# Two post-norm layers on one core: the mLSTM's gates on four column groups, its state parts first, and eight heads' scores on four row groups

## The chip, the cores and the metric

One core of a Trainium2 chip runs the whole program. The metric is the device time in microseconds; the time quoted for a kernel is the median of its runs. A profile is one execution, recorded instruction by instruction. PE is TensorE's matmuls, PEld its weight loads, DVE VectorE, ACT ScalarE, POOL GpSimd and SP the sync engine, which issues most DMAs here. L69 means line 69 of the kernel before.

## The reference

Input x is 4 x 256 tokens of 256 features. Four sub-layers follow, each as `x = layernorm(x + f(x))`: softmax attention with 16 heads and rotary parts; a gated network of width 1024 with a Walsh-Hadamard transform; an mLSTM block that has a gated network inside; and a gated network with int8 weights. The change touches the third:

```python
q, k, v = h_in @ wq, h_in @ wk, h_in @ wv        # h_in = rmsnorm(x) * norm1_w; 8 heads, dqk 16, dv 32
i_pre, f_pre = softcap(h_in @ w_ig + b_ig), softcap(h_in @ w_fg + b_fg)   # cap 15, tanh
Fcum = cumsum(log_sigmoid(f_pre))
Dmat = Fcum[s] - Fcum[t] + i_pre[t], and -inf where t > s
m = max_t(Dmat)
C = (q @ k.T) / sqrt(dqk) * exp(Dmat - m)
n = max(|sum_t C|, exp(-m))
h = (C / n) @ v                                   # per head, then an RMS norm per head
x1 = x + (sigmoid(o_pre) * h_norm) @ w_out
out = x1 + (silu(h2 @ w_gate) * (h2 @ w_up)) @ w_down     # h2 = rmsnorm(x1) * norm2_w
```

## The kernel before

All arithmetic of this part is fp32. The 1024 tokens are worked in two halves of 512 (two batches of 256 each), called n = 0 and 1, so that one half's mLSTM ("mixing phase") runs beside the other half's gated network.

The program is written in order, and the order written is a priority: at compile time a scheduler puts each engine's instructions in a fixed order, taking the first written one that is ready in its own reckoning. Each engine then runs its list in order and waits on semaphores. `issue_after(x)` keeps an instruction behind x on x's engine.

The interleaving is written with generators. `merge(first, other)` runs the mixing phase; where it yields a number of microseconds, that much of the other half's network is written in between. The network (`glu`, `down`) yields 1.7 after each piece of TensorE work: 16 such units in `glu` (a gate or an up product of 128 hidden rows), then 8 in `down`, 24 in all. These units are called filler below. What remains of them is written after the next norm.

PSUM has eight banks. The networks take turns on four ("d"), the mixing phase on the other four ("m").

A mixing phase, `mlstm(n)`:

- `mlstm_in` normalises (9.0 us of filler meanwhile), transposes to feature-major `fm`, and computes the gate pre-activations `w_if` (L69, from L622): gate g and batch bb give 32 output columns each, batch bb on PSUM partitions 32 bb to 32 bb + 31, gate g in columns of its own. Two tanh instructions follow, then `gates`: log-sigmoid, scans and maxima on ACT and DVE. The running maximum `gmax` is stored to DRAM as `far` (L689, SP).
- Queries and keys (`w_qk`), then four products for values and output gate (`w_vo`), then `by_token` (L704), which transposes the gate rows into `tok`, and keys by token (`ks`).
- `within(t, bb, half)`, four times: loads `far` of four heads, broadcast to all partitions, as `wide` (L740, SP, 512 KB), computes scores for four heads with 32-row matmuls on two row groups (L747) into two banks, subtracts `wide` from the mask on POOL (L756), takes eight exponentials on ACT (L763), and multiplies scores and exponentials on DVE (L767).
- `between` (L714, L726): the state that the first 128 tokens of a batch leave to the second, in two matmuls.
- `attend` (L778), a half behind: exponentials times values; an ACT copy and a DVE add take it out of PSUM.
- `head_norm`, once a batch: a chain of some twenty small steps on ACT and DVE that ends with `xs` (L808).
- The result is transposed and multiplied by `w_out` (L850), and L851 adds the residual. The next network's norm follows, with 6.0 us of filler, then its transposes, and then what is left of the filler.

Of the kernel before, what the change touches and what calls it, by code (L numbers as in the profile page):

```python
# [9 lines left out]
F32 = mybir.dt.float32  # L10
# [3 lines left out]
ALU = mybir.AluOpType  # L14
AX = mybir.AxisListType

P = 128
# [21 lines left out]
def tile_two_layers(ctx: ExitStack, tc: tile.TileContext, a: dict, out: bass.AP):  # L39
# [6 lines left out]
    def bank(tag):  # L46
        return psum.tile([P, 512], F32, tag=tag, name=f"ps_{tag}")
# [18 lines left out]
    def mm_k(ps, lhs, rhs, n):  # L66

        for i in range(n):
            nc.tensor.matmul(ps, lhsT=lhs(i), rhs=rhs(i), start=(i == 0), stop=(i == n - 1))  # L69

# [398 lines left out]
    nc.sync.dma_start(w_if[:, :, 0:40], a["w_if"])  # L469
    b_if = late.tile([64, 2], F32, tag="b_if", name="b_if")  # L470
    nc.gpsimd.memset(b_if, 0.0)
    for bb in range(2):
        for g in range(2):
            nc.sync.dma_start(b_if[32 * bb : 32 * bb + H1, g : g + 1], a["b_if"][32 * g : 32 * g + H1, :])
    vecs = load("vecs", [P, 6])
# [53 lines left out]
    def transposed(src, dst, tag, weight=None):  # L529
# [11 lines left out]
        return evicted  # L541

    def glu(xT, wg, wu, hT, tag):

        for c in range(NH):
            cols = slice(c * P, (c + 1) * P)
            pg, pu = bank(tag), bank(tag)
            mm_k(pg, lambda i: wg[:, i, cols], lambda i: xT[:, i, :], KC)
            yield 1.7
            mm_k(pu, lambda i: wu[:, i, cols], lambda i: xT[:, i, :], KC)  # L550
            g = work.tile([P, HALF], F32, tag="glu_g", name="glu_g")
            nc.scalar.activation(g, pg, AF.Tanh, scale=0.5)  # L552
            nc.vector.scalar_tensor_tensor(g, g, 1.0, pg, ALU.add, ALU.mult)
            nc.vector.tensor_tensor(hT[:, c, :], pu, g, ALU.mult)
            yield 1.7

    def down(hT, wd, j, tag, rows):

        po = bank(tag)[:, :D]
        for i in range(NH):  # L560
            nc.tensor.matmul(  # L561
                po, lhsT=hT[:, i, j * P : (j + 1) * P], rhs=wd[:, i, :], start=(i == 0), stop=(i == NH - 1)
            )
            if i == NH // 2 - 1:
                yield 1.7
        nc.vector.scalar_tensor_tensor(rows, po, 0.5, rows, ALU.mult, ALU.add)
        yield 1.7
# [35 lines left out]
    nc.gpsimd.memset(ones, 1.0)  # L603
    bias = mix.tile([2 * 32, 2], F32, tag="bias", name="bias")
    nc.scalar.mul(bias, b_if, 1.0 / CAP)
# [7 lines left out]
    def mlstm_in(n, t):  # L613
# [7 lines left out]
        pg = bank("m")  # L621
        for g in range(2):  # L622
            for bb in range(2):
                mm_k(
                    pg[32 * bb : 32 * bb + 32, g * S : (g + 1) * S],
                    lambda i: w_if[:, i, 32 * g : 32 * g + 32],
                    lambda i: fm[:, i, bb * S : (bb + 1) * S],
                    KC,
                )
        gt = mix.tile([64, 2, S], F32, tag="gt", name="gt")  # L630
        for g in range(2):
            nc.scalar.activation(
                gt[:, g, :], pg[:64, g * S : (g + 1) * S], AF.Tanh,
                bias=bias[:, g : g + 1], scale=1.0 / CAP,
            )
        gates(n, t, gt)
        yield 0.0
        pq, pk = bank("m"), bank("m")
        mm_k(pq, lambda i: w_qk[:, i, 0, :], lambda i: fm[:, i, :], KC)
        mm_k(pk, lambda i: w_qk[:, i, 1, :], lambda i: fm[:, i, :], KC)  # L640
        qT = mix.tile([P, HALF], F32, tag="qT", name=f"qT{n}")
# [5 lines left out]
        nc.gpsimd.memset(va[:, :, :, DV1], 1.0)  # L647
        sig = mix.tile([P, NJH, D], F32, tag="sig", name=f"sig{n}")
        for j in range(NJH):
            pv = bank("m")  # L650
            mm_k(pv, lambda i: fm[:, i, j * P : (j + 1) * P], lambda i: w_vo[:, i, :], KC)
            nc.scalar.copy(va[:, j, :, 0:DV1], pv[:, 0:D].rearrange("p (h d) -> p h d", h=H1))
            nc.scalar.activation(sig[:, j, :], pv[:, D:], AF.Tanh, scale=0.5)
        t.update(va=va, sig=sig, qT=qT, kT=kT)
        yield 1.0
        by_token(n, t)
        pt = bank("m")
# [16 lines left out]
    def gates(n, t, gt):  # L674
# [6 lines left out]
        neg = mix.tile([64, 1], F32, tag="neg", name="neg", bufs=2)  # L681
        nc.scalar.activation(lsp, gt[:, 1, :], AF.Exp, scale=-CAP)
        nc.scalar.activation(lsp, lsp, AF.Ln, bias=1.0)
        nc.vector.tensor_tensor_scan(fcum, ones, lsp, 0.0, ALU.mult, ALU.subtract)
        nc.vector.scalar_tensor_tensor(g, gt[:, 0, :], CAP, fcum, ALU.mult, ALU.subtract)
        nc.vector.tensor_tensor_scan(gmax, g, g, -3.0e38, ALU.max, ALU.max)
# [48 lines left out]

    def within(t, bb, half):


        wide = mix.tile([P, HG, S], F32, tag="wide", name="wide", bufs=2)
        nc.sync.dma_start(wide, t["far"][bb, half * HG : (half + 1) * HG].partition_broadcast(P))  # L740
        ps = (bank("m"), bank("m"))
        for odd in range(2):
            for c in range(2):
                for k in range(2):
                    rows = slice(32 * (2 * half + k), 32 * (2 * half + k) + 32)
                    tok = slice(bb * S + c * P, bb * S + (c + 1) * P)
                    nc.tensor.matmul(  # L747
                        ps[k][:, (2 * odd + c) * P : (2 * odd + c + 1) * P],
                        lhsT=t["kT"][rows, odd, tok], rhs=t["qT"][rows, tok],
                        start=True, stop=True,  # L750
                    )
        out = []
        for k in range(2):
            h = 4 * half + 2 * k
            ex = mix.tile([P, 4, P], F32, tag="ex", name="ex", bufs=4)
            nc.gpsimd.tensor_tensor(  # L756
                ex, mask.unsqueeze(1).to_broadcast([P, 4, P]),
                wide[:, 2 * k : 2 * k + 2, :].rearrange("p h (c s) -> p (h c) s", c=2), ALU.subtract,
            )
            for odd in range(2):  # L760
                for c in range(2):
                    at = 32 * bb + h + odd
                    nc.scalar.activation(  # L763
                        ex[:, 2 * odd + c, :], ex[:, 2 * odd + c, :], AF.Exp,
                        bias=t["tok"][:, c, 0, at : at + 1],
                    )
            nc.vector.tensor_tensor(  # L767
                ex, ps[k].rearrange("p (x s) -> p x s", x=4), ex, ALU.mult
            )
            out.append(ex)  # L770
        return out

    def attend(t, bb, half, exs, part, hv):

        ph = bank("m")
        for c in range(2):
            for x in range(HG):
                nc.tensor.matmul(  # L778
                    ph[:, (c * HG + x) * DV : (c * HG + x + 1) * DV],
                    lhsT=exs[x // 2][:, 2 * (x % 2) + c, :], rhs=t["va"][:, 2 * bb + c, half * HG + x, :],  # L780
                    start=True, stop=True,
                )
        heads = slice(half * HG, (half + 1) * HG)
        by_h = ph[:, : 2 * HG * DV].rearrange("p (c h d) -> p c h d", c=2, h=HG)
        nc.scalar.copy(hv[:, 0, heads, :], by_h[:, 0])
        nc.vector.tensor_tensor(hv[:, 1, heads, :], by_h[:, 1], part[:, heads, :], ALU.add)

    def head_norm(n, t, bb, hv):
# [18 lines left out]
        )  # L807
        nc.vector.scalar_tensor_tensor(  # L808
            hos[n][:, 2 * bb : 2 * bb + 2, :], t["sig"][:, 2 * bb : 2 * bb + 2, :], 1.0,
# [3 lines left out]
    def run(stream):  # L813
        for _ in stream:
            pass

    def take(count, stream):
        return itertools.islice(stream, count)

    def mlstm(n):  # L820

        t, waiting = {}, []

        def finish():
            bb, half, exs, hv = waiting.pop()
            attend(t, bb, half, exs, t["part", bb], hv)
            if half == 1:
                head_norm(n, t, bb, hv)

        yield from mlstm_in(n, t)  # L830
        for bb in range(2):
            hv = mix.tile([P, 2, H1, DV], F32, tag="hv", name="hv", bufs=2)
            for half in range(2):
                exs = within(t, bb, half)
                if half == 0:
                    carried = between(t, bb)
                run(take(1, carried))
                yield 1.5
                if waiting:
                    finish()  # L840
                waiting.append((bb, half, exs, hv))
        yield 3.0
        finish()
        yield 6.0
        fm = feature_major(n)
# [273 lines left out]
```

## Time and profile before

| | |
|---|---|
| median of 3 runs | 731.13 us (730.96 to 732.91) |
| the profiled execution | 732.8 us |
| its span | 731.0 us |
| granted TensorE clock | 0.997 of full |
| busy: PE, PEld | 719.4, 485.1 us |
| busy: DVE, ACT, POOL | 398.8, 238.8, 175.1 us |
| mixing phase 0, first gate matmul to the next network | 492.97 to 557.47 us |
| mixing phase 1, the same | 571.14 to 636.09 us |

A row of the order of time has the start, the length, the engine, the line, the operation, what it writes and reads, the shape and how many records were merged into it. In brackets stand the idle time ahead of it and what ended that. A matmul's modelled end overlaps the next one's start, so a row's true share is the distance to the next row's start. The rows that the prediction rests on are shown there.

### The profile page before, as it was taken

Reading aid. Unit: us, or ns where it says so; the run is one execution under the profiler, and the core shown is the slowest. Engines: PE = TensorE matmul, PEld = TensorE weight load, DVE = VectorE, ACT = ScalarE, POOL = GpSimd, SP = SyncE. Lnnn points to the kernel's source line nnn. Section 1 sums busy time; section 2 is a strip of 40 time slices with the busy share of each in tenths; the row PEclk is TensorE's granted clock in tenths of the full one; section 3 lists DMA queues with packets and bytes.
Section 4 is the critical chain, followed back from the end, with each engine's and each line's share of the span. In section 5 each row is a group of like instructions: output and inputs, shape, how many; then the busy total and the mean of one; then the engine's idle time right before and its main releaser. Section 6 shows DMA issues by size and latency. Waiting matters only on the chain.

```text
span 731.0 us, 8563 instructions
## 1 busy us (share of the span) xinstructions
PE 719.4 (98%) x2956; PEld 485.1 (66%) x2956; DVE 398.8 (55%) x1017; ACT 238.8 (33%) x625; POOL 175.1 (24%) x187
## 2 busy tenths in 40 slices
PE   8999999999999999999999999999999999999995
PEld 4667667667767767766766774655776476747885
DVE  0373544545655364364455555373778458754766
ACT  2232422432342242243233332126521452111553
POOL 0812422439440341243044000002300050000210
PEclk9999999999999999999999999999999999999998
DMA  8542042183133223322311313002130020000001
GB/s 247 212 107 56 18 123 56 25 279 61 29 101 58 44 87 59 62 79 48 72 30 30 58 60 66 0 1 64 55 115 1 23 94 1 0 1 0 1 1 57
DMA packets 48107, 45.34 MB, mean 62 GB/s; under 512 B 9504, under 2 KB 42688, under 8 KB 46016
## 3 DMA queue, kind: packets, MB, share of 16 engines
q1 hardware_dynamic: 46928, 40.47, 21.1%
q0 software_dynamic: 432, 3.15, 1.2%
q10 hardware_dynamic: 704, 1.18, 0.5%
q8 instruction: 23, 0.38, 0.2%
q14 instruction: 20, 0.16, 0.1%
HBM read 25.61 MB, written 1.08 MB: 37 GB/s over the span
## 4 chain that ended last, share of the span: by engine, by line
PE 91%; DVE 4%; ACT 2%; DMA 1%; issue 1%; POOL 0%; DVEq 0%; ACTq 0%
PE ps_mm L69 37%; PE ps_d L69 11%; PE ps_ot L69 8%; PE ps_m L69 8%; PE ps_d L561 5%; PE ps_pt L232 4%; PE ps_sc L232 4%; PE ps_d L861 4%; PE ps_sc L241 2%; PE ps_m L561 2%; PE ps_m L778 2%; PE ps_pt L241 2%; PE ps_mm L185 1%; DMA w_qkv<-in_w_qkv 1%; PE ps_m L534 1%; ACT ex L763 1%
## 5 line engine op out<-in xcount | busy, mean ns | idle before, releaser
L69 PE MATMUL ps_mm<-xT,w_qkv 128*128 128x512 f32 x248 | 115.8, 593 | 0.0
L176 POOL TENSOR_TENSOR rope_raw<-rope_raw,cst 128x512 f32<-128x512 f32 x32 | 40.7, 1271 | 231.8 <-DVE rope_swp L173 224.5
L260 ACT ACTIVATE pr<-ps_sc,nmax 128x256 f32<-128x256 f32 x64 | 29.5, 472 | 142.2 <-DVE nmax L251 142.2
L69 PEld LDWEIGHTS ps_mm<-xT,w_qkv 128*128 128x128 f32 x248 | 47.0, 190 | 37.2 <-issue 33.8
L69 PEld LDWEIGHTS ps_ot<-prT,v 128*128 128x128 f32 x240 | 45.6, 190 | 28.8 <-issue 25.4
L69 PE MATMUL ps_ot<-prT,v 128*128 128x256 f32 x240 | 60.8, 379 | 0.0
L69 PE MATMUL ps_mm<-w_o,oT 128*128 128x256 f32 x256 | 60.6, 380 | 0.0
L69 PE MATMUL ps_mm<-xT,w_rot 128*128 128x512 f32 x128 | 59.0, 604 | 0.0
L270 DVE TENSOR_SCALAR pr<-pr,rinv 128x256 f32<-128x256 f32 x128 | 57.8, 485 | 1.8
L69 PE MATMUL ps_mm<-w_qkv,xT 128*128 128x256 f32 x256 | 58.1, 379 | 0.3 <-ACT kn L198 0.3
L69 PE MATMUL ps_d<-fm,w 128*128 128x512 f32 x128 | 56.7, 594 | 0.3 <-ACT fm L538 0.3
L69 PEld LDWEIGHTS ps_mm<-w_o,oT 128*128 128x128 f32 x256 | 48.4, 190 | 12.9 <-issue 6.0
L69 PEld LDWEIGHTS ps_mm<-w_qkv,xT 128*128 128x128 f32 x256 | 48.6, 190 | 8.1 <-issue 1.0
L251 DVE TENSOR_REDUCE nmax<-ps_sc 128x2 f32<-128x512 f32 x32 | 20.6, 687 | 59.1 <-PE ps_sc L241 59.1
L756 POOL TENSOR_TENSOR ex<-cst,wide 128x512 f32<-128x512 f32 x16 | 19.9, 1264 | 131.7 <-DMA wide<-far 71.0
L210 DVE COPY v<-ps_mm 128x512 f32<-128x512 f32 x32 | 22.0, 691 | 50.4 <-PE ps_mm L69 46.8
L268 DVE RECIPROCAL rinv<-rsum 128x2 f32<-128x2 f32 x64 | 9.7, 152 | 64.2 <-ACT pr L260 64.0
L278 DVE STREAM_TRANSPOSE cross<-pr 128x512 f32<-128x512 f32 x60 | 42.7, 711 | 1.5
L69 PEld LDWEIGHTS ps_d<-fm,w 128*128 128x128 f32 x128 | 24.0, 190 | 27.1 <-issue 24.9
L69 PEld LDWEIGHTS ps_mm<-xT,w_rot 128*128 128x128 f32 x128 | 23.2, 189 | 28.1 <-issue 20.4
L177 POOL TENSOR_TENSOR rope_swp<-rope_swp,cst 128x512 f32<-128x512 f32 x32 | 40.8, 1275 | 0.0
L552 ACT ACTIVATE glu_g<-ps_d 128x512 f32<-128x512 f32 x24 | 14.2, 592 | 67.4 <-PE ps_d L69 67.4
(197 smaller groups left out, 1191.2 us busy)
## 6 DMA issues: line engine op xcount, KB each, us to landing
prT<-cross SPq DMA_DIRECT2D x240, 64.0 KB, 2.1
w_qkv<-in_w_qkv SPq DMA_DIRECT2D x7, 1024.0 KB, 5.1
wide<-far SPq DMA_DIRECT2D x8, 512.0 KB, 4.3
w<-in_w SPq DMA_DIRECT2D x3, 1024.0 KB, 12.7
w_o<-in_w_o SPq DMA_DIRECT2D x8, 256.0 KB, 3.1
acc<-in_x SPq DMA_DIRECT2D x2, 512.0 KB
w_gate<-in_w_gate SPq DMA_DIRECT2D x1, 1024.0 KB, 8.5
w_up<-in_w_up SPq DMA_DIRECT2D x1, 1024.0 KB, 10.4
```

The lines of the kernel that those rows point to most:

```text
L69: nc.tensor.matmul(ps, lhsT=lhs(i), rhs=rhs(i), start=(i == 0), stop=(i == n - 1))
L176: nc.gpsimd.tensor_tensor(by_b(raw), by_b(raw), cs, ALU.mult)
L177: nc.gpsimd.tensor_tensor(by_b(swp), by_b(swp), sn, ALU.mult)
L210: return nc.vector.tensor_copy(v[:, 2 * jj : 2 * jj + 2, :], ps.rearrange("p (t d) -> p t d", t=2))
L232: nc.tensor.matmul(ps[bb][e][:, qt * S : (qt + 1) * S], lhsT=qn[:, e, queries(bb, qt)], rhs=kn[:, e, keys(bb)], start=(qt == 0), stop=Fals ...
L241: nc.tensor.matmul(ps[bb][e][:, qt * S : (qt + 1) * S], lhsT=qr[rows, queries(bb, qt)], rhs=kr[rows, keys(bb)], start=False, stop=(qt == 1 ...
L251: nc.vector.tensor_reduce(nmax, ps.rearrange("p (t k) -> p t k", t=2), AX.X, ALU.max, negate=True)
L260: nc.scalar.activation(pr[:, qt, :], ps[:, qt * S : (qt + 1) * S], AF.Exp, bias=nmax[:, qt : qt + 1], accum_out=rsum[:, qt : qt + 1],)
L270: nc.vector.tensor_scalar(pr[:, qt, :], pr[:, qt, :], rinv[:, qt : qt + 1], None, ALU.mult)
L278: return nc.vector.transpose(cross[:, :, e], pr.rearrange("p t (x i) -> p x t i", i=32))
L561: nc.tensor.matmul(po, lhsT=hT[:, i, j * P : (j + 1) * P], rhs=wd[:, i, :], start=(i == 0), stop=(i == NH - 1))
L861: nc.tensor.matmul(ps, lhsT=lhs, rhs=rhs, start=(k == 0), stop=(k == len(terms) - 1))
```

## The change

Five things change.

- **Gates.** Gate g and batch bb get PSUM partitions from 64 g + 32 bb on, so that the four products lie on four column groups and share the same 256 PSUM columns. The loop over the two halves of the contraction is outermost. One tanh of 128 partitions replaces two of 64. Queries and keys are held behind the last gate matmul.
- **Distances.** `wide` is gone. `far` is loaded straight into `ex` (two loads a batch, both batches at once, right after the gates), and POOL subtracts it from the mask in place.
- **Order.** `by_token` and the keys by token come ahead of the last value product. The state parts of both batches come next, with a filler unit after each of the two steps. `decays` (the exponentials, eight at a time) is written ahead of the scores that need it, behind the network's latest tanh.
- **Scores.** `within` computes a batch's eight heads in one go on four row groups into four banks; two filler units follow; then both halves of `attend`.
- **Down evictions.** The network's `down` results are taken out of PSUM behind the last instruction of the latest `head_norm`. The yield ahead of the output product is 9.0, not 6.0.

By the numbers yielded, a phase now asks for 33.3 us of filler up to its output product, and asked for 28.4 before.

```diff
-    b_if = late.tile([64, 2], F32, tag="b_if", name="b_if")
+    b_if = late.tile([P, 1], F32, tag="b_if", name="b_if")
...
+    evictions = []
+    chained = []
...
-            nc.scalar.activation(g, pg, AF.Tanh, scale=0.5)
+            evictions.append(nc.scalar.activation(g, pg, AF.Tanh, scale=0.5))
...
-        nc.vector.scalar_tensor_tensor(rows, po, 0.5, rows, ALU.mult, ALU.add)
+        with tc.issue_after(chained[-1].ins) if chained else contextlib.nullcontext():
+            nc.vector.scalar_tensor_tensor(rows, po, 0.5, rows, ALU.mult, ALU.add)
...
-        for g in range(2):
-            for bb in range(2):
-                mm_k(
-                    pg[32 * bb : 32 * bb + 32, g * S : (g + 1) * S],
-                    lambda i: w_if[:, i, 32 * g : 32 * g + 32],
-                    lambda i: fm[:, i, bb * S : (bb + 1) * S],
-                    KC,
-                )
-        gt = mix.tile([64, 2, S], F32, tag="gt", name="gt")
...
+        for i in range(KC):
+            for g in range(2):
+                for bb in range(2):
+                    at = 64 * g + 32 * bb
+                    gated = nc.tensor.matmul(
+                        pg[at : at + 32, 0:S], lhsT=w_if[:, i, 32 * g : 32 * g + 32],
+                        rhs=fm[:, i, bb * S : (bb + 1) * S], start=(i == 0), stop=(i == KC - 1),
+                        skip_group_check=True,
+                    )
+        gt = mix.tile([P, S], F32, tag="gt", name="gt")
+        nc.scalar.activation(gt, pg[:, 0:S], AF.Tanh, bias=bias, scale=1.0 / CAP)
         gates(n, t, gt)
+        for bb in range(2):
+            distances(t, bb)
         yield 0.0
         pq, pk = bank("m"), bank("m")
-        mm_k(pq, lambda i: w_qk[:, i, 0, :], lambda i: fm[:, i, :], KC)
-        mm_k(pk, lambda i: w_qk[:, i, 1, :], lambda i: fm[:, i, :], KC)
+        with tc.issue_after(gated.ins):
+            mm_k(pq, lambda i: w_qk[:, i, 0, :], lambda i: fm[:, i, :], KC)
+            mm_k(pk, lambda i: w_qk[:, i, 1, :], lambda i: fm[:, i, :], KC)
...
         for j in range(NJH):
+            if j == NJH - 1:
+                by_token(n, t)
+                keys_by_token(n, t, fm)
             pv = bank("m")
...
-        yield 1.0
-        by_token(n, t)
+        decays(t, 0, 0)
...
+    def distances(t, bb):
+        ex = mix.tile([P, H1, 2, P], F32, tag="ex", name="ex", bufs=2)
+        for half in range(2):
+            heads = slice(half * HG, (half + 1) * HG)
+            nc.sync.dma_start(
+                ex[:, heads].rearrange("p h c s -> p h (c s)"), t["far"][bb, heads].partition_broadcast(P)
+            )
+        for r in range(HG):
+            two = ex[:, 2 * r : 2 * r + 2].rearrange("p h c s -> p (h c) s")
+            nc.gpsimd.tensor_tensor(
+                two, mask.unsqueeze(1).to_broadcast([P, 4, P]), two, ALU.subtract
+            )
+        t["ex", bb] = ex
+
+    def decays(t, bb, half):
+        ex = t["ex", bb]
+        with tc.issue_after(evictions[-1].ins):
+            for h in range(half * HG, (half + 1) * HG):
+                for c in range(2):
+                    at = 32 * bb + h
+                    nc.scalar.activation(
+                        ex[:, h, c, :], ex[:, h, c, :], AF.Exp, bias=t["tok"][:, c, 0, at : at + 1]
+                    )
+
+    def within(t, bb):
+        ps = [bank("m") for _ in range(HG)]
         for odd in range(2):
             for c in range(2):
-                for k in range(2):
-                    rows = slice(32 * (2 * half + k), 32 * (2 * half + k) + 32)
+                for r in range(HG):
+                    rows = slice(32 * r, 32 * r + 32)
                     tok = slice(bb * S + c * P, bb * S + (c + 1) * P)
                     nc.tensor.matmul(
-                        ps[k][:, (2 * odd + c) * P : (2 * odd + c + 1) * P],
+                        ps[r][:, (2 * odd + c) * P : (2 * odd + c + 1) * P],
                         lhsT=t["kT"][rows, odd, tok], rhs=t["qT"][rows, tok],
                         start=True, stop=True,
                     )
+        for r in range(HG):
+            two = t["ex", bb][:, 2 * r : 2 * r + 2].rearrange("p h c s -> p (h c) s")
+            nc.vector.tensor_tensor(
+                two, ps[r].rearrange("p (x s) -> p x s", x=4), two, ALU.mult
+            )
...
     def mlstm(n):
+        t = {}
         yield from mlstm_in(n, t)
+        carried = [between(t, bb) for bb in range(2)]
+        for k, _ in enumerate(zip(*carried)):
+            yield 1.7
+            if not k:
+                decays(t, 0, 1)
         for bb in range(2):
             hv = mix.tile([P, 2, H1, DV], F32, tag="hv", name="hv", bufs=2)
+            within(t, bb)
+            if not bb:
+                decays(t, 1, 0)
+            yield 3.4
             for half in range(2):
+                attend(t, bb, half, hv)
+            if not bb:
+                decays(t, 1, 1)
+                yield 1.7
+            chained.append(head_norm(n, t, bb, hv))
+        yield 9.0
-        yield 3.0
-        finish()
-        yield 6.0
         fm = feature_major(n)
```

## The prediction

> **What bounds the kernel now.** I read the page's rows by engine first, then the busy time of the two stretches that the change touches, then TensorE's order of time in the first of them, and then the other engines' order of time at the same place.
>
> ```profile
> PE 719.4 (98%) x2956; PEld 485.1 (66%) x2956; DVE 398.8 (55%) x1017; ACT 238.8 (33%) x625; POOL 175.1 (24%) x187
> PE 91%; DVE 4%; ACT 2%; DMA 1%; issue 1%; POOL 0%; DVEq 0%; ACTq 0%
> 492.97:557.47 64.50, 64.19 (x323) 43.03 (x323) 40.58 (x113) 25.49 (x71) 11.19 (x11) 1.00 0.19 66
> 571.14:636.09 64.95, 64.53 (x328) 43.62 (x327) 41.13 (x125) 25.50 (x71) 9.93 (x8) 1.00 0.10 33
> ```
>
> TensorE is busy 98% of the span and is 91% of the chain that ended last. In the two rows of stretches (length, then PE, PEld, DVE, ACT, POOL, granted clock) it idles 0.31 and 0.42 us, at full clock. Each stretch runs from a mixing phase's first gate matmul to the first matmul of the next feed-forward network. So the time falls by what TensorE is relieved of there, as long as it still finds work at every step.
>
> ```profile
> 492.97 0.62 PE L69 MATMUL ps_m<-fm,w_if 128*32 128x256 f32 x2
> 493.52 1.13 PE L69 MATMUL ps_m<-fm,w_qk 128*128 128x512 f32 x2
> 494.57 1.92 PE L69 MATMUL ps_m<-fm,w_if 128*32 128x256 f32 x14
> 496.42 2.84 PE L69 MATMUL ps_m<-fm,w_qk 128*128 128x512 f32 x6
> 499.10 7.03 PE L69 MATMUL ps_m<-w_vo,fm 128*128 128x512 f32 x16
> ...
> 507.66 1.16 PE L747 MATMUL ps_m<-qT,kT 32*128 32x128 f32 x16
> 508.75 0.71 PE L714 MATMUL ps_m<-va,ks 128*128 128x264 f32 x2
> ...
> 512.51 0.68 PE L726 MATMUL ps_m<-state,qT 128*128 128x264 f32 x2 [0.19 <-DVE ex L767]
> 513.03 1.88 PE L69 MATMUL ps_d<-fm,w 128*128 128x512 f32 x4
> 514.74 1.87 PE L778 MATMUL ps_m<-va,ex 128*128 128x33 f32 x16
> ```
>
> First column: start; a row lasts until the next begins. Each fp32 matmul is two records. Gates (w_if, 32 output columns) take 0.55 + 1.85 us and are split around a query matmul; one pass of scores (L747) takes 1.09 us and there are four per phase. The ps_d rows are the other half-batch's network, 1.72 us per unit of four records: the filler.
>
> **The gates.** Full-width 128x256 records follow each other at 0.216 us (42 in 9.06 us, chain). The x14 row fits matmuls that start in order with two column groups open: 8 steps of 0.216 plus 0.12 for entering and leaving; x2 is 2 steps plus 0.12. After, four groups are open and the contraction half is outermost: 16 records in 4 steps, 0.98 us. The queries and keys then run in one piece: 8 records, 3.54 us instead of 1.05 + 2.68. Stretch to 499.10: 6.13 before, 4.52 after. **-1.6 us a phase.** If the second half of fm (DVE, two evictions in 1.40 us) is late for the second half of the gates, a value matmul may slip between, +0.2; the queries may not, they are held behind the last gate, and nothing else queues for that.
>
> **The scores.** One pass is 8 steps of 0.112 us (the attention matmuls, 16 in 1.80 us, have that pace too) plus 0.2, with two row groups at once. With four, a batch's 32 records need the same 8 steps: 1.11 us. Two passes of 1.09 fall away per phase, and with each 0.1 us of the next matmul's slower start (L714's first record takes 0.33 us before its second starts, where 0.22 is the pace). **-2.35 us a phase.** The stall in the L726 row and the slowed pass before it cost 0.3 us, in the second phase 0.85 (a score pass of 1.77 us and 0.18 idle). They come from multiplications (L767) that wait for exponentials; the new order has the exponentials done earlier. **-0.3 and -0.85.** Two attention halves in one piece save about 0.15 at each join, -0.3 a phase.
>
> Here a rule speaks for less: the Trainium skill, "TensorE: Matmul & The Clock Gate", Part 3 (packing small matmuls), gives 3.07x as measured for four row tiles, not 4x. This trace shows only pairs, at the full 2x. By the rule the scores take 1.37 us and the gates 1.25: 4 x 0.26 + 2 x 0.27 = 1.6 us less gain in all. I take the trace's pace and keep the 1.6 for the range. If the array ran no more than two at once, gates and scores would gain nothing; that is a rival below.
>
> **What is moved.**
>
> ```profile
> 502.50 0.64 SPq L689 DMA_DIRECT2D far<-gmax  x2
> 503.82 9.23 SPq L740 DMA_DIRECT2D wide<-far  x4
> 507.76 4.95 POOL L756 TENSOR_TENSOR ex<-cst,wide 128x512 f32<-128x512 f32 x4 [71.01 <-DMA wide<-far]
> 516.25 2.49 POOL L756 TENSOR_TENSOR ex<-cst,wide 128x512 f32<-128x512 f32 x2 [3.54 <-PE ps_m L778]
> 509.05 4.96 ACT L763 ACTIVATE ex<-ex,tok 128x128 f32<-128x128 f32 x16 [2.23 <-POOL ex L756]
> ```
>
> Gates end 2.4 us earlier and are one tanh of 0.43 us, not two in 0.83: gmax is written near 499, the two 8 KB stores land 1.3 us later, and SP issues four loads of 512 KB at once. Before, the first landed 3.9 us after issue and two took 5.1 us; four should be in 9 us after about 500, and the last two no longer wait for a buffer. Nothing else is queued on SP. POOL then runs eight subtractions of 1.26 us back to back, about 504 to 514; behind them lie the memset of va and the int8 weights' DMA issues (536 before), far off. Exponentials: 32 x 0.31 = 10 us of ACT a phase as before; batch 0's end near 511.5 to 512 where the scores now stand at 512 to 513. So 0. Each set of eight is put behind the network's latest tanh on ACT, which is 0.59 us and done by then: 0. The next tanh (L552) may queue behind eight exponentials, 2.5 us; its bank has a second pair, so 0, but 1 us each if the loads are late.
>
> Putting the state parts first moves 4 x 0.55 us of PE within the phase: 0. Moving the by-token transposes ahead of the last value product needs their rows by 502.7; I get 501.5 to 502.6 (two table loads of 1.28 us included): 0 to +0.5, taken as 0.
>
> Second rule, against the change: the skill's "TensorEngine Tiling (Array Packing)", PSUM Bottleneck, says that tiling speeds up TensorE but not the emptying of PSUM. Here four banks fill in 1.11 us and DVE needs 4 x 0.69 = 2.8 us. Bare, the first attention half would wait for two multiplications, 1.5 us for each of four batches, 6 us in all. But two filler units (3.44 us) stand between, so I take 0; the third and fourth end 0.6 us before the units do.
>
> **The filler's budget.** There are 24 units of 1.7. By the yields the phase asked for 17 of them before its output product, now 20; the four after that cover the norm, so none is left behind its transposes, where 22 records (4.75 us) stood.
>
> ```profile
> 541.03 0.69 DVE L808 SCALAR_TENSOR_TENSOR xs<-sig,hh 128x512 f32<-128x512 f32 x1
> 541.64 0.42 DVE L566 SCALAR_TENSOR_TENSOR acc<-ps_d,acc 128x256 f32<-128x256 f32 x1
> 546.80 4.48 PE L561 MATMUL ps_d<-w,hT 128*128 128x256 f32 x20
> 551.33 1.56 PE L534 MATMUL ps_d<-cst,h 128*128 128x128 f32 x8
> 552.72 4.91 PE L561 MATMUL ps_d<-w,hT 128*128 128x256 f32 x22
> ```
>
> The uncovered eviction (0.75 us, of which the other four transposes hide some) costs 0.4 us in the first phase. In the second, before already had nothing there but four transposes. The head norm takes 9.7 us (attention ends 532.0, xs at 541.7) against five units, 8.6 us, plus transposes; then product to norm's end is 5.1 us against 6.9 minus what was pulled forward. After the last attention the supply is 10 units, 17.2 us, plus 5.5 of the phase's own transposes and products, 22.7; the need is about 9.6 (norm) + 0.6 (transposes) + 0.7 (eviction) + 3.5 (product) + 5.1 (second norm) + 1 (transposes) = 20.5. Slack: 2 us. The down eviction kept behind the norm saves it up to 0.8 us of DVE and holds one of four banks: 0.
>
> **Sum.** First phase: -1.6 - 2.35 - 0.3 - 0.3 + 0.4 + 0.2 = -3.95. Second: -1.6 - 2.35 - 0.85 - 0.3 + 0.2 = -4.9. Together -8.9; I give back 0.9 for waits of a new order. **-8 us.** The profiled execution is 732.8 (span 731.0): it goes to 724.8. The median of the runs shown, 731.13, is 1.7 below that execution: 723.1. What a measurement here can tell from no change is about 0.3%, 2.2 us.
>
> **The rivals.**
> 1. Part of it is lost to new waits (0.16): loads, POOL and ACT run 2 us late, or the slack goes, in both phases. For: the loads now compete with each other, and in the first phase the same chain made the only stalls. Against: it starts 4 us earlier. It gives back 2.5 to 5.5: 725.5 to 728.5.
> 2. Four tiles run as two (0.08). Nothing in the trace shows more than two. Of the gates' and scores' 7.9 us only some 0.5 for the unsplit queries stays; with the rest of the sum that is -1.5: 729.6, no change.
> 3. Slower (0.08): the filler runs out. If the head norm ends later than the 2 us of slack allow, TensorE waits in each phase with nothing left. Before had 22 records in hand. For: DVE is busy 23.3 of the 30 us from 520 to 550, and batch 0's norm now shares it with all four multiplications of batch 1. With no cover at all the chain from product to transposes is bare: 5.1 + 1.7 = 6.8 a phase, +13.6 - 8.9: 736. It turns slower where both norms end over 6.5 us late, near 546. Against: I add only 1 us of overlap.
>
> The likeliest case has 0.68 (720.8 to 725.5). Chances: faster 0.84, same 0.08, slower 0.08. The range takes in the first rival: 720.8 to 728.3.
>
> **What would show it.** Right: the gate records in one block of about 1.0 us; 32 score records in about 1.1; subtractions and exponentials ahead of the scores; TensorE idle under 1 us in each phase; each stretch about 4 to 5 us shorter. Wrong: score blocks near 2 us (rival 2), idle PE before attention named after ex (1), or idle PE before the transposes of h or after them (3).

## The result and the profile after

| | median | lowest to highest | runs |
|---|---|---|---|
| before | 731.65 us | 730.46 to 732.91 | 6 |
| after | 723.33 us | 722.07 to 729.0 | 6 |

The ratio of after to before is 0.99, interval 0.9877 to 0.9923. The profiled execution of after is the slowest of its six (729.0 us, span 727.2), so a second profile of the same kernel, taken with the experiments (722.25 us, span 720.4), is read beside it.

The rows by engine and the chain's shares of after:

```profile
PE 716.1 (98%) x2956; PEld 483.3 (66%) x2956; DVE 397.2 (55%) x1017; ACT 237.2 (33%) x623; POOL 174.8 (24%) x187
PE 94%; DVE 4%; ACT 1%; DMA 1%; issue 0%; ACTq 0%; DVEq 0%
```

TensorE bounds the kernel more than before. The two mixing phases, from the first gate matmul to the first matmul of the next network (stretch, length, busy PE, PEld, DVE, ACT, POOL, granted clock, DMA share, GB/s), first in this profile and then in the second one of the same kernel:

```profile
492.78:557.28 64.50, 64.10 (x323) 43.08 (x322) 38.63 (x110) 24.80 (x70) 11.10 (x11) 0.92 0.18 66
572.75:632.28 59.53, 59.53 (x323) 40.90 (x322) 39.15 (x123) 24.09 (x69) 9.86 (x8) 0.97 0.11 37
```

```profile
492.62:552.19 59.57, 59.17 (x323) 40.39 (x322) 38.51 (x110) 24.80 (x70) 11.09 (x11) 1.00 0.20 72
567.65:625.51 57.86, 57.86 (x323) 40.11 (x322) 39.03 (x123) 24.08 (x69) 9.85 (x8) 1.00 0.10 38
```

Both are one program with one order of work. In the first profile phase 0 is exactly as long as before (64.50 us) and in the second it is 4.93 shorter. The difference is in the column of the granted clock, the third number from the right: 0.92 and 0.97 in the one, 1.00 in the other. The windows of the first profile around the two attention blocks of phase 0, cut where the clock changes:

```profile
515.24:518.66 3.42, 3.42 (x29) 3.11 (x28) 3.00 (x6) 1.58 (x5) 0.00 (x0) 1.00 0.00 0
518.66:525.48 6.82, 6.82 (x44) 4.06 (x43) 3.24 (x10) 1.13 (x3) 0.00 (x0) 0.50 0.00 0
525.48:528.89 3.41, 3.41 (x12) 1.61 (x9) 3.27 (x13) 0.60 (x1) 0.00 (x0) 1.00 0.00 0
528.89:532.31 3.42, 3.42 (x32) 3.31 (x30) 2.98 (x7) 0.27 (x1) 0.00 (x0) 1.00 0.02 7
532.31:535.72 3.41, 3.41 (x8) 1.85 (x8) 1.42 (x4) 0.50 (x2) 0.15 (x1) 0.50 0.00 0
```

TensorE is busy all the time (in each row the length and the busy time of PE, the first two numbers behind the stretch, are equal), yet its clock is halved for two windows of 3.41 us and then for a third. A fourth lies in phase 1 (597.16 to 600.58). Together the phases and the stretch between them are 6.62 us longer than in the second profile: 1.65 a window.

TensorE's order of time in phase 0 of the first profile of after (start, us, operation, records):

```profile
492.78 1.07 PE L633 MATMUL ps_m<-fm,w_if 128*32 128x256 f32 x16
493.78 3.70 PE L70 MATMUL ps_m<-fm,w_qk 128*128 128x512 f32 x8
497.32 5.31 PE L70 MATMUL ps_m<-w_vo,fm 128*128 128x512 f32 x12
...
505.79 1.05 PE L726 MATMUL ps_m<-va,ks 128*128 128x264 f32 x4
506.68 1.88 PE L70 MATMUL ps_d<-fm,w 128*128 128x512 f32 x4
508.40 1.05 PE L738 MATMUL ps_m<-state,qT 128*128 128x264 f32 x4
...
511.10 1.17 PE L783 MATMUL ps_m<-qT,kT 32*128 32x128 f32 x32
512.20 3.70 PE L70 MATMUL ps_d<-fm,w 128*128 128x512 f32 x8
515.74 4.21 PE L799 MATMUL ps_m<-va,ex 128*128 128x33 f32 x32
519.75 3.76 PE L70 MATMUL ps_d<-fm,w 128*128 128x512 f32 x4
523.45 2.09 PE L783 MATMUL ps_m<-qT,kT 32*128 32x128 f32 x32
525.47 3.70 PE L70 MATMUL ps_d<-fm,w 128*128 128x512 f32 x8
...
557.28 1.98 PE L70 MATMUL ps_d<-fm,w_gate 128*128 128x512 f32 x4 [0.41 <-DVE fm L543]
```

The gates are one block of 1.00 us (492.78 to 493.78), a batch's 32 score records take 1.10 (511.10 to 512.20), and no wait stands before scores or attention. What a halved window does is seen from 519.75 on: the network unit there lasts 3.70 where an undisturbed one takes 1.72, and batch 1's scores last 2.02 instead of 1.10. Ahead of it, at 515.74, stand 32 attention matmuls of 33 columns, unbroken for 3.5 us and more. Whether they are the cause, the experiments have to show.

POOL, ACT and DVE at the same place:

```profile
504.30 9.85 POOL L758 TENSOR_TENSOR ex<-cst,ex 128x512 f32<-128x512 f32 x8 [67.73 <-DMA ex<-far]
507.31 5.94 ACT L770 ACTIVATE ex<-ex,tok 128x128 f32<-128x128 f32 x20
541.84 0.69 DVE L830 SCALAR_TENSOR_TENSOR xs<-sig,hh 128x512 f32<-128x512 f32 x1
542.45 0.42 DVE L573 SCALAR_TENSOR_TENSOR acc<-ps_d,acc 128x256 f32<-128x256 f32 x1
```

Eight subtractions run from 504.30 to 514.15 (forecast 504 to 514). Batch 0's exponentials are done ahead of its scores' end. The first eviction of `down`'s results starts 0.6 us after xs, as it did before the change, where nothing held it.

### The profile page after: what moved, and what is told of

Its sections match the earlier page's. It is cut to its first block, busy times and chain, and to the rows that moved or that the text cites. A ratio compares the mean times of both kernels' runs of the same rounds, so it can differ in the third digit from the quotient of the medians.

```text
span 727.2 us, 8550 instructions
## 1 busy us (share of the span) xinstructions
PE 716.1 (98%) x2956; PEld 483.3 (66%) x2956; DVE 397.2 (55%) x1017; ACT 237.2 (33%) x623; POOL 174.8 (24%) x187
## 4 chain that ended last, share of the span: by engine, by line
PE 94%; DVE 4%; ACT 1%; DMA 1%; issue 0%; ACTq 0%; DVEq 0%
PE ps_mm L70 37%; PE ps_d L70 11%; PE ps_m L70 8%; PE ps_ot L70 8%; PE ps_d L567 6%; PE ps_pt L234 4%; PE ps_sc L234 4%; PE ps_d L880 4%; PE ps_sc L243 2%; PE ps_m L799 2%; PE ps_m L567 2%; PE ps_pt L243 2%; PE ps_mm L187 1%; PE ps_m L783 1%; PE ps_m L537 1%; DMA w_qkv<-in_w_qkv 1%
## 5 line engine op out<-in xcount | busy, mean ns | idle before, releaser
L70 PE MATMUL ps_d<-fm,w 128*128 128x512 f32 x128 | 60.2, 624 | 0.3 <-ACT fm L541 0.3
L758 POOL TENSOR_TENSOR ex<-cst,ex 128x512 f32<-128x512 f32 x16 | 19.7, 1260 | 113.5 <-DMA ex<-far 113.5
```

What stands on the lines that cost most here:

```text
L70: last = nc.tensor.matmul(ps, lhsT=lhs(i), rhs=rhs(i), start=(i == 0), stop=(i == n - 1))
```

## The experiments

All times are medians with lowest and highest, in us. Three groups of kernels ran, each beside runs of before: 732.37 (730.73 to 734.17), 732.0 (730.23 to 733.12) and 730.92 (729.97 to 732.88). Ratios are to those.

Three questions were open. Do the gains come from the four tiles? What halves the clock: too little streaming in the window before, or the packing of four tiles at once? (The recorded expectations call these theory A and theory B.) And what do the cover between scores and attention, and the held evictions, do?

**The changed kernel beside the others.** No edit.

> The changed kernel again. Both theories have to explain that its runs spread from 722 to 729 us and that the profiled one shows the TensorE clock halved in four windows of 3.41 us. Theory A (too little activity): a batch's 32 attention matmuls (L799, 33 columns each, paced by their weight loads) now stand in one block of 3.5 us or more, and a clock window that falls on it finds the array mostly still; the next window runs at half clock. Then the halved stretches begin inside or right after L799 rows, there are 0 to 4 of them in a run, and the mean clock is 0.997 less 0.0024 for each. Theory B (too much packing): four tiles at once bring the clock down. Then the halved stretches follow the score or gate blocks (L783, L633). Time 722 to 725 in most runs.

725.01 (723.62 to 729.47), ratio 0.9908 (0.9883 to 0.9933). No run reached clock 0.997, which before has: 723.72, 725.91 and 726.08 us came with 0.993, 729.47 with 0.988. The profiled one has two halved windows, each behind an attention block, and at one of them the scores were half caught:

```profile
513.78 3.68 PE L799 MATMUL ps_m<-va,ex 128*128 128x33 f32 x32
517.30 3.26 PE L70 MATMUL ps_d<-fm,w 128*128 128x512 f32 x4
520.49 1.50 PE L783 MATMUL ps_m<-qT,kT 32*128 32x128 f32 x32
```

**A unit of the network before each half of the attention**, instead of two ahead of both.

```
-            yield 3.4
             for half in range(2):
+                yield 1.7
                 attend(t, bb, half, hv)
```

> One of the two filler units that stand between a batch's scores and its attention is moved between the two halves of the attention; the count of units is the same. Theory A: no block of attention is longer than 1.8 us, so the clock stays at 0.997 in all runs, the runs draw together, and the time is 721.5 to 722.5, about 1 us under the median of the changed kernel. Theory B: the scores and gates are packed as before, so halved windows remain and the spread stays 722 to 729. If one unit (1.72 us) is too short for the first two multiplications (1.4 us), up to 0.5 us a batch comes back, 2 us in all.

726.02 (724.47 to 729.87), ratio 0.993 (0.9908 to 0.9952). The clock was 0.993 to 0.997 in five runs of six (0.988 in the other), better than the changed kernel's, but the time was not. The profiled run has no halved window. TensorE's order of time, then its waits (us in total, times, longest), show why it is still slow:

```profile
510.34 1.98 PE L70 MATMUL ps_d<-fm,w 128*128 128x512 f32 x4
...
513.54 2.19 PE L799 MATMUL ps_m<-va,ex 128*128 128x33 f32 x16 [1.21 <-DVE ex L790]
```

```profile
PE ps_m L799 <- DVE ex L790: 2.4, 3, 1.2
```

With one unit between scores and attention, TensorE waits for DVE's second multiplication of the scores. That is the bare wait which the prediction put at 1.5 us and held covered by two units: with two it does not appear, with one it is up to 1.2. Theory A's forecast for this run, 0.997 in all runs, missed: three of the six stand at 0.988 to 0.995. An idle 1.2 us with an attention half of 1.8 us behind it is again some 3 us in which little streams, which would fit theory A; none of those three runs was profiled, so this is not shown.

**Tiles in pairs.** Each gate tile's two contraction halves follow each other, and the scores run on row groups 0 and 1, then 2 and 3.

```
-        for i in range(KC):
-            for g in range(2):
-                for bb in range(2):
+        for g in range(2):
+            for bb in range(2):
+                for i in range(KC):
...
-        for odd in range(2):
-            for c in range(2):
-                for r in range(HG):
+        for pair, odd, c in itertools.product(range(2), range(2), range(2)):
+                for r in (2 * pair, 2 * pair + 1):
```

> The changed kernel with the gate and score matmuls in an order that leaves only two tiles open at once (gates: contraction innermost; scores: row groups 0 and 1, then 2 and 3). If four tiles ran at twice the pace of two, the gate block grows from 1.00 to 1.86 us and a score block from 1.10 to 2.0: 2 x 0.86 + 4 x 0.9 = 5.3 us slower, about 728. If four never ran at once, no change. Theory A: halved clock windows remain, since the attention block is as it was. Theory B: they go, and the mean clock is 0.997 in all runs.

724.95 (723.36 to 725.59), ratio 0.9894 (0.9876 to 0.9912), where 728 was expected: a miss. TensorE's order of time shows why:

```profile
490.86 0.62 PE L633 MATMUL ps_m<-fm,w_if 128*32 128x256 f32 x2
491.41 1.12 PE L70 MATMUL ps_d<-fm,w 128*128 128x512 f32 x2
492.46 1.08 PE L633 MATMUL ps_m<-fm,w_if 128*32 128x256 f32 x14
493.48 3.70 PE L70 MATMUL ps_m<-fm,w_qk 128*128 128x512 f32 x8
...
509.94 1.72 PE L782 MATMUL ps_m<-qT,kT 32*128 32x128 f32 x32
511.59 3.70 PE L70 MATMUL ps_d<-fm,w 128*128 128x512 f32 x8
```

The gates' x14 takes 1.02 us (492.46 to 493.48) with the contraction innermost, where before needed 1.85 for x14 in its own layout. In the layout of before, 16 records share two column groups, 8 steps of 0.216 each; here each of four groups has 4. So the column positions set the pace and not the order of the loops: tiles run beside each other even when one tile's records stand together in the program. The scores in pairs take 1.65 us, between 1.10 and the 2.0 expected: 4 x 0.55 = 2.2 us of the 2.98 by which the stretch from phase 0's first gate to the end (230.80 us) is longer than in the changed kernel's undisturbed profile (227.82). The medians are nonetheless equal (724.95 and 725.01): here no window was halved (clock 0.997 to 0.998), while the changed kernel's runs beside it stood at 0.993 or lower. At this point that spoke for the packing as the cause.

**The gates alone**, put into the kernel before: four column groups, the contraction outermost, one tanh, queries held behind the last gate; nothing else.

```
-                    pg[32 * bb : 32 * bb + 32, g * S : (g + 1) * S],
...
+        for i in range(KC):
+            for g in range(2):
+                for bb in range(2):
+                    at = 64 * g + 32 * bb
+                    gated = nc.tensor.matmul(
+                        pg[at : at + 32, 0:S], lhsT=w_if[:, i, 32 * g : 32 * g + 32],
...
+        with tc.issue_after(gated.ins):
+            mm_k(pq, lambda i: w_qk[:, i, 0, :], lambda i: fm[:, i, :], KC)
```

> The kernel before with the gates' part of the change alone (four column groups, contraction outermost, one tanh, queries held behind the last gate). By the prediction's term: -1.6 us a phase, -3.2 in all, 728.2. Rival: what the gates give up is lost again at the score stalls behind them (0.3 and 0.85 us in before), or the split of the queries was free: -1.5 or less. No halved clock windows in either theory's reading of A; in B perhaps some after the gates.

728.04 (726.73 to 728.55), ratio 0.9941 (0.9926 to 0.9956). The time expected, 728.2, came, but the gain did not: 4.3 us under the runs of before beside it, where 3.2 was expected. Phase 0 is 62.63 us and phase 1 62.53: 1.87 and 2.42 less than before. The gates give 1.6 of each. The rest is about what was put on the stalls behind the exponentials (0.3 and 0.85): gates that end some two microseconds earlier are enough to remove them, without the new order.

```profile
492.67 1.07 PE L628 MATMUL ps_m<-fm,w_if 128*32 128x256 f32 x16
509.22 1.16 PE L747 MATMUL ps_m<-qT,kT 32*128 32x128 f32 x16
510.31 0.71 PE L726 MATMUL ps_m<-state,qT 128*128 128x264 f32 x2
```

The second score pass now runs at 1.09 us, and the state product behind it starts with no wait.

**Down evictions not held** behind the head norm's chain.

```
-        with tc.issue_after(chained[-1].ins) if chained else contextlib.nullcontext():
+        if True:
```

> The changed kernel with the down evictions not held behind the head norm. The prediction put that hold at 0 to 0.8 us of DVE time, inside the slack. If slack covers it: no change against e0_after (725.0). If the norm chain is what TensorE waits for before its last products: up to 0.8 us a phase slower, 1.6 in all. The clock as in e0_after, two halved windows in most runs (0.993).

725.44 (722.04 to 729.01), ratio 0.9916 (0.9892 to 0.9941): the same as the changed kernel. Its profile has four halved windows like after's, and from phase 0's first gate to the end it takes 234.38 us against 234.44. The hold is worth nothing that shows.

**Attention halves with work between** (the split kernel). In batch 0 the last value product goes between them, in batch 1 a unit of the network; one unit less follows, so that the budget stays.

```
...
+        t["values"] = values
+        for j in range(NJH - 1):
+            if j == NJH - 2:
+                by_token(n, t)
+                keys_by_token(n, t, fm)
+            values(j)
...
             for half in range(2):
+                if half and bb:
+                    yield 1.7
+                elif half:
+                    t["values"](NJH - 1)
                 attend(t, bb, half, hv)
...
-        yield 9.0
+        yield 7.3
```

> The changed kernel with both attention blocks split: the last value product moves between the two halves of batch 0's attention (by-token transposes one value product earlier), and one filler unit between those of batch 1; two units stay ahead of each first half, so that no multiplication is late. Theory A (too little activity in a clock window): a window now holds at most 1.75 us of attention and 1.66 us of dense work, an activity near 0.55, where halved windows so far followed 0.36 or less; the clock stays at 0.997 in every run, and the time falls by the two windows' 1.7 us each, to 721 to 722.5. Theory B (four tiles at once): scores and gates are packed as in the change, so halved windows remain, 0.993, 724 to 726.

723.26 (721.55 to 724.27), ratio 0.9891 (0.9873 to 0.9909), where 721 to 722.5 was expected; clock 0.996 to 0.998 in every run. The four-tile scores and gates are all there, so packing does not bring the halving by itself:

```profile
511.77 1.87 PE L803 MATMUL ps_m<-va,ex 128*128 128x33 f32 x16
513.48 1.96 PE L70 MATMUL ps_m<-w_vo,fm 128*128 128x512 f32 x4
515.28 1.87 PE L803 MATMUL ps_m<-va,ex 128*128 128x33 f32 x16
...
580.89 1.75 PE L787 MATMUL ps_m<-qT,kT 32*128 32x128 f32 x32
```

The split is not free: from phase 0's first gate to the end it takes 229.24 us, 1.4 more than an undisturbed changed kernel (227.82). One score block in phase 1 takes 1.7 again, and there are waits for xs that the changed kernel lacks.

**One more network unit between the halves**, in both batches, with nothing else moved.

```
             for half in range(2):
+                if half:
+                    yield 1.7
                 attend(t, bb, half, hv)
```

> The changed kernel with one edit: one more filler unit, between the two halves of each batch's attention. Theory A: clock 0.997 in every run, as in e5_vo_split. But two of a phase's 24 units are used before the last attention, 3.4 us, and the slack behind it was reckoned at 2 us: TensorE should wait 1 to 1.7 us a phase near the transposes of h, so 722.5 to 724.5. Theory B: 0.993 and those waits on top, 727 to 728.

724.61 (723.67 to 729.07), ratio 0.9915 (0.9893 to 0.9937). Five runs kept the clock, one did not (0.989). The two units per phase are missing at its end. The waits:

```profile
PE ps_d L70 <- DVE fm L543: 0.7, 1, 0.7
PE ps_d L537 <- DVE h L528: 0.4, 1, 0.4
PE ps_m L537 <- DVE h L528: 0.4, 1, 0.4
PE ps_m L70 <- DVE fm L543: 0.3, 1, 0.3
PE ps_m L799 <- DVE ex L790: 0.3, 1, 0.3
```

This is the filler's slack: two units (3.4 us) are more than is left. At the end of the phases TensorE waits 1.2 and 0.7 us, where the changed kernel waits 0.4 and nothing, so an estimated 2.6 us were left, in line with the 2 us that the prediction gave it. The run that lost the clock goes against theory A's forecast, and was not profiled.

**Pairs, and a longer stretch of short matmuls.** The kernel in pairs, without the unit between batch 0's attention and batch 1's scores.

```
                 decays(t, 1, 1)
-                yield 1.7
```

> e2_pairs (two tiles open at once), with the filler unit between batch 0's attention and batch 1's scores taken out, so that 3.5 us of attention and 1.65 us of scores stand in one block. Theory A: some window lies wholly in that block at any phase of the free-running window, so at least one halved window a phase, 0.993 or lower in every run, although nothing runs more than two at once; 725 to 729. Theory B: the clock is 0.997 in all runs, as it was in e2_pairs, and the time 724 to 726.

729.44 (727.5 to 731.68, 22 runs), ratio 0.9974 (0.9964 to 0.9983). The clock was 0.989 to 0.993, where all five runs of the first kernel in pairs had 0.997 or 0.998. Its windows:

```profile
524.42:527.84 3.42, 3.42 (x30) 3.31 (x30) 3.15 (x16) 0.79 (x3) 0.07 (x1) 1.00 0.02 7
527.84:531.25 3.41, 3.41 (x5) 1.33 (x4) 1.22 (x4) 0.32 (x2) 0.09 (x1) 0.50 0.00 0
...
592.69:596.10 3.41, 3.41 (x45) 3.37 (x46) 0.93 (x4) 0.77 (x3) 0.00 (x0) 1.00 0.00 0
596.10:602.93 6.83, 6.83 (x22) 3.51 (x18) 5.71 (x18) 0.63 (x1) 0.00 (x0) 0.50 0.00 0
```

No four tiles run at once in these scores, and the clock is halved three times. So four tiles at once are not needed for the halving, and by the split halves above they are not enough for it. The lack of streaming is the cause that fits; what it leaves open stands in the last section.

**Three more.** The split kernel with a further unit after the second state step, the changed kernel again, and the split kernel again, side by side.

The first of the three has this beyond the split kernel's edit:

```
-            yield 1.7
+            yield 3.4 if k else 1.7
             if not k:
```

> e5_vo_split with one more filler unit ahead of batch 0's scores, since in its second phase those took 1.75 us, waiting for banks, where 1.10 is the pace. Theory A: the clock stays at 0.997. If a unit is still to spare behind the last attention, 0.65 us come off; if not, TensorE waits there as in e6_split_units and the sum is 0 to +1 us. Against the changed kernel on the same chip: 1 to 3 us faster.

> The changed kernel once more, beside e10_vo_split_again on one chip. Theory A: halved windows in nearly every run (clock 0.993 or below, 1.7 us each), median 723 to 725.5.

> e5_vo_split once more, on the same chip as the changed kernel. Theory A: no halved window in any run, and the median 1 to 2.5 us under that of e9_after_again. If the split costs as much as the halved windows, no difference.

| kernel | median (lowest to highest) | ratio (interval) | clock of the runs |
|---|---|---|---|
| split, a unit more ahead | 723.45 (722.84 to 723.74) | 0.9895 (0.9878 to 0.9912) | 0.996 to 0.997 |
| changed, again | 725.73 (722.13 to 730.58) | 0.9927 (0.9898 to 0.9956) | 0.983 to 0.997 |
| split, again | 721.97 (721.6 to 723.26) | 0.9881 (0.9865 to 0.9897) | 0.996 to 0.998 |

The changed kernel's own runs line up by the clock: 722.13 and 722.25 us at 0.997, 725.47 and 725.99 at 0.992 and 0.993, 730.58 at 0.983. The split kernel beats before and the changed kernel in this set: its interval lies just below the changed kernel's, and its spread is 1.7 us instead of 8.5 (over 4 runs and 8). From phase 0's first gate to the end its profile is 1.4 us longer than the changed kernel's at its best (229.20 us against 227.82); it wins because none of its runs shows a halved clock. Its first set of runs stood at 723.26. The further unit ahead takes 0.4 us off that stretch (228.81 us; 0.65 was expected), which the medians do not show.

## Why the prediction was right, point by point

The mechanism was right: TensorE was the bound, and the time fell by what it was relieved of in the two phases. That 723.33 came so close to 723.1 is luck. The sum behind it holds two errors that offset each other: the phases lost 10.2 us where 8.9 stood, and halved clock windows, which the sum does not have, took 0 to 6.6 us back. Profile against profile, without halved windows, 724.8 was forecast and 722.25 measured. Phase 0, worked out from the starts in TensorE's order of time, before against the undisturbed profile of after:

| part of phase 0 | before | after | measured | in the prediction's sum |
|---|---|---|---|---|
| gates, queries, keys, values | 13.09 | 11.51 | -1.58 | -1.6, and +0.2 for a slipped product |
| transposes by token | 1.60 | 1.50 | -0.10 | none |
| scores with the stall | 4.67 | 2.21 | -2.46 | -2.35 - 0.3 |
| state products | 2.17 | 1.78 | -0.39 | 0 ("moved") |
| attention | 7.01 | 6.98 | -0.03 | -0.3 with the next row |
| 36 records of network between them | 15.70 | 16.01 | +0.31 | |
| norm's transposes, down and output products, to the next network | 20.26 | 19.59 | -0.67 | +0.4 |
| sum | 64.50 | 59.57 | -4.93 | -3.95 |

(The parts add to -4.92 by rounding.) Phase 1 lost 7.09 us, of which 1.79 is a network unit that went to the stretch ahead of it: -5.30 against -4.9. Both together make the -10.2.

- **Gates: right in size, wrong in its model.** 1.59 us a phase. "Matmuls that start in order with two column groups open" is refuted by the kernel in pairs: the loop order could have been the other one at the same pace. The gain is in the four positions. The value matmul that might slip between (+0.2) did not.
- **Scores: right.** 1.10 us for 32 records against 1.11. The Trainium skill's 3.07x ("TensorE: Matmul & The Clock Gate", Part 3), measured there for four row tiles and 512 columns, by which the prediction estimated 1.37 for them and 1.25 for the gates, did not hold here: 1.10 and 1.00. The pace of the trace before did.
- **Stalls behind the exponentials: right in size.** -0.3 and -0.85 went. The prediction gave this to the new order of the exponentials; the gates alone removed them.
- **State products: mis-sized.** Two pairs in 0.89 each instead of four in about 0.54: 0.39 a phase that "4 x 0.55 us of PE moved: 0" missed.
- **Joins of attention: wrong by about 0.6.** Neither attention nor the units around it became shorter; the joins went from between attention halves to between units and score or attention blocks.
- **The end of the phase: wrong by 1.07, to the good side.** The wait for fm came as forecast (0.41 against 0.4), but the transposes ahead of it took 0.35 less, so that both together cost 0.06. And the 64 down records ran in three unbroken pieces, 13.81 us, where before three of four pieces had 0.61 of extra time at their ends. The prediction counted the wait that was new and not the pieces that were joined.
- **Cover of the scores' multiplications: right.** Two units hide it; with one, 1.2 us shows.
- **Filler's slack of 2 us: in line with the runs.** Not one wait of the changed kernel inside a phase; with two units fewer, 0.3 to 0.7 in each place.
- **Held evictions: 0, right.**
- **The 0.9 given back "for waits of a new order": wrong in kind.** Waits took 0.41 and 0.30 us. What was given back was the clock: none to four windows in the profiles, 1.65 us each. The undisturbed profile is 722.25, and the medians of the three sets of runs of this kernel, 723.33, 725.01 and 725.73, stand 1 to 3.5 above it. Single runs reached 729.0, 729.47 and 730.58, beyond the range's upper end of 728.3, which was put there for late loads. No rival named this loss, because the search for new costs went through waits and engines and not through what TensorE itself streams.

The three rivals fell: no new wait before attention, no score block of 2 us at full clock, no idle TensorE at the transposes beyond 0.41.

## What to carry to other kernels

When a change gathers short matmuls in one block, compare not only the records but the granted clock over the block's surroundings: a block of 3.5 us that streams little can cost the next 3.4 us half their pace, although TensorE is shown busy throughout. Put long matmuls between the halves of such a block. And cost the joins of a reordered phase from the starts of the rows, end to end, or small pieces (here 0.1 to 0.7 us each) are missed in both directions.

## What the runs showed of the hardware that was not expected

**A halved clock with no idle time.** In these traces the clock is 1.00 or 0.50 within the kernel's body, in windows of 3.41 us. The Trainium skill ("TensorE: Matmul & The Clock Gate", Part 1) states both, and that the grid of windows runs free of the kernel's start. The traces agree: the first halved window begins at 518.66 us in one profile of this program and at 517.82 in another, and profiles have none, two or four. What the page speaks of is idle windows, and by that none here would be halved: the rows show 3.42 of 3.42 us busy. The attention matmuls follow each other at about 0.11 us, the pace of their weight loads (28 loads fill 3.11 of 3.42 us), while 33 columns stream for an estimated 0.03 (from 512 columns in 0.43 us, and twice that at half clock). Estimated so for a window, the share of time in which the array streams, weighted with the part of the array in use, is:

```
kernel             window             estimated share   clock in the next window
after              528.89 to 532.31   0.28              0.50
after              593.75 to 597.16   0.31              0.50
e0_after           514.40 to 517.82   0.33              0.50
e7_pairs_long      524.42 to 527.84   0.33              0.50
after              515.24 to 518.66   0.36              0.50
e9_after_again     525.06 to 528.47   0.38              1.00
e2_pairs           526.59 to 530.00   0.40              1.00
e0_after           524.64 to 528.06   0.43              1.00
before, lowest     519.08 to 522.50   0.46              1.00
split, lowest      524.79 to 528.20   0.60              1.00
```

So in these runs the border lies between 0.36 and 0.37 of this estimate: of all windows at full clock between 480 and 640 us in the thirteen profiles, the ten with 0.27 to 0.36 were followed by a halved one, and no other was (the lowest of these, 0.37, is in the pairs' longer kernel). Before splits its attention in halves of 1.8 us, which cannot fill a window; the change joins them to 3.5 us, which can, where the grid falls so. Dense weight loads alone are not the mark: the kernel with one more unit has them for 3.18 of 3.42 us (530.02 to 533.44), with more streaming beside them, and keeps its clock.

Laid over a kernel's own profile at every position that the grid can take, the estimate tells which kernels can be caught. Before never falls below 0.37 and the split kernels never below 0.57, and none of their runs (51 runs beside the experiments, and 13) is under clock 0.996. The pairs' longer kernel has a window under 0.37 at every position, and all its 22 runs were slowed. The changed kernel has one at some five positions in six, and 15 of its 20 runs were slowed (clock 0.995 or lower). Two kernels do not fit. The first one in pairs has such a window at two positions in three (the lowest in its profile was 0.40), yet five runs of five kept the clock; the one with one more unit at none, yet one run of six did not. So it is not excluded that the packing has some part in the halving.

Windows that were halved already came back to full clock at 0.78 and above, and not at 0.73 and below (0.72 in after, 518.66 to 522.07). What the hardware really counts was not measured; the estimate only sorts these windows.

**Tiles do not wait for program order.** The gate tiles of the kernel in pairs show it (1.02 us for 14 records); its scores overlap in part (1.65 us, between 1.10 and 2.0).

**The start of phase 0 moves**, from 490.5 to 491.3 us in some profiles to 492.3 to 493.1 in others, in code ahead of everything that was touched and at the same clock. Before's runs gather near 730.4 and 732.6, about as far apart; only one of them was profiled, so that this is their spread is not shown, and the cause was not looked for. Stretches from phase 0's first gate on are free of it, which is why the comparisons above use them.
